# Graph convolution: 32 list entries of each step fetched as single rows by ScalarE's transfers

## The chip, the cores and the metric

The kernel runs on one core of a Trainium2 chip. The core has five engines, each with an instruction queue of its own: TensorE (PE; its weight loads are PEld) multiplies matrices, VectorE (DVE) and ScalarE (ACT) work element by element, GpSimd (POOL) issues the indirect gathers here, SyncE (SP) issues plain transfers. Transfers between the main memory and the core's memory (SBUF) run on 16 DMA engines and report on semaphores. PSUM is the small memory that TensorE writes. The metric is device time in microseconds of one execution.

## What is computed

The graph has N = 50,000 nodes with 128 features each and a list of 1,650,000 edges, sorted by destination. Each node has an edge to itself in the list. A message is one of two linear maps of the source's row, by the type of the edge; messages are summed by destination, the node's own linear map is added, then ReLU, the residual and a normalisation without scale.

```python
Xs = X[src]
m_data = Xs @ W_data.T + b_data
m_ctrl = Xs @ W_control.T + b_control
msg = jnp.where((edge_types == 0)[:, None], m_data, m_ctrl)
agg = jax.ops.segment_sum(msg, dst, num_segments=X.shape[0])
out = jax.nn.relu(agg + (X @ W_self.T + b_self))
return _layernorm(X + out, axis=-1)
```

## The kernel before

Because the maps are linear, the kernel sums source rows first, once for each edge type, and multiplies by the weights once per node. The sorted list is cut into blocks (`NBLK`, 448 of them) and each block into `Q` = 2 steps. A step has `R` = 14 chunks of 128 list entries (`SIZES`), and `F` = 53 further entries, the fillers. The entries that are a node's edge to itself need no fetch, because the block's own rows are in SBUF anyway (`xT`); `fill` puts the step's fillers at their places in the chunks, so that a gather has no idle row. A full block thus takes `BE` = 2 x (1792 + 53) = 3690 entries. Block 0 and the last one are plain: they have no fillers. The last one takes what remains of the list (`REST`, 686 entries, six chunks).

For each chunk, GpSimd issues one indirect gather of 128 rows of 512 bytes (`gathers`, line 507), at the indices in one column of an SBUF tile. VectorE builds a matrix of ones and zeros for all chunks of a block (`onehot`, line 482): row = entry, column = the destination's place in a window of 64 nodes, twice, for the two edge types. TensorE multiplies the gathered rows by it (`products`, line 530) and accumulates a step's 14 chunks in PSUM. `counts` (line 490) sums the same matrix over the chunks, for the bias terms. `add` adds the step's sums to the block's window of nodes (line 539), `layer` multiplies by the weights (lines 559 to 569), `moments`, `root` and `store` normalise (`root` is a square root on ScalarE, line 595, once for two blocks; `store` begins on VectorE with line 601), and `store_rows` writes the rows from SyncE's queue (line 609) at a row number held in a register.

The order of the work on every engine is written out by hand: within one engine, instructions run in the order in which the Python code emits them. The main loop runs over blocks b. At its start it emits the next edge lists (every ten blocks, `load_edges`, on SyncE), the adds of block b-1, then the one-hot matrix and counts of block b+2 (`AHEAD` = 2). The gathers and products of block b follow in four passes of seven chunks; between the passes stand the fillers of a later block (`fill`, lines 370 to 391, up to `RAHEAD` = 5 blocks ahead), `layer` and `moments` of block b-1, `positions` and, every ten blocks, `columns`, which prepares what ten blocks need on VectorE. The gathers of a step share one of `SLOTS` = 5 buffers and one semaphore, for which TensorE waits before the step's first product (line 514). The last block has passes of two chunks, each with a buffer of its own.

Register values are read from SBUF by a load instruction on the queue that uses them: `window` (line 458, SyncE, nine registers every eight blocks, for the transfer of line 465 and the stores) and `positions` (VectorE, four registers a block). `find_bad` makes a flag at the end; line 1006 loads it on every engine, and the path in `general` runs only where it isn't zero.

The tiles `m`, `new` and `old` of `fill` have a buffer each, of 128 partitions x (28 chunks x 63).

Of the kernel before, what the change touches and what calls it, by code (L numbers as in the profile page):

```python
# [11 lines left out]
F32 = mybir.dt.float32  # L12
BF16 = mybir.dt.bfloat16
U8 = mybir.dt.uint8
I32 = mybir.dt.int32
AF = mybir.ActivationFunctionType
ALU = mybir.AluOpType
AX = mybir.AxisListType
SP = mybir.EngineType.SP
DVE = mybir.EngineType.DVE  # L20

N = 50000
D = 128
ROW = 4 * D
E = 1650000
P = 128
# [6 lines left out]
R = 14  # L33
W = 64
Q = 2
# [3 lines left out]
F = 53  # L39
LATE = 10  # L40
FX = LATE + F
R1 = R
H = R + 1
C1 = Q * R1
SIZES = [P] * R
SIZE = sum(SIZES)
CE = Q * SIZE
BE = CE + Q * F
NBLK = 2 + (E + LATE - CE) // BE
REST = E + LATE - CE - (NBLK - 2) * BE  # L50
REST_ROWS = [min(n, max(0, REST - q * SIZE - sum(SIZES[:r]))) for q in range(Q) for r, n in enumerate(SIZES)]
# [2 lines left out]
GB = 10  # L54
GROUPS = -(-NBLK // GB)
GC = GB * C1
AHEAD = 2
SLOTS = 5
RAHEAD = 5
LOOP = 2048.0  # L60
COLS = 256
# [24 lines left out]
def plain(b):  # L86

    return b == 0 or b >= NBLK - 1
# [3 lines left out]
    return bass.AP(tensor=ap.tensor, offset=ap.offset, ap=[[0, n], *ap.ap])  # L92


def straight(ctx, tc, c, x, x_t, edges_t, edges_f, dst_first, first_p, out):

# [13 lines left out]
    eds = ctx.enter_context(tc.tile_pool(name="eds", bufs=2))  # L112
    ohp = ctx.enter_context(tc.tile_pool(name="ohp", bufs=AHEAD + 1))
    gat = ctx.enter_context(tc.tile_pool(name="gat", bufs=SLOTS))
    fil = ctx.enter_context(tc.tile_pool(name="fil", bufs=2))
    stp = ctx.enter_context(tc.tile_pool(name="stp", bufs=3))
    ps = ctx.enter_context(tc.tile_pool(name="ps", bufs=2, space=bass.MemoryType.PSUM))
# [59 lines left out]
    nc.vector.memset(stats, 0.0)  # L177
    most = keep.tile([P, GROUPS], F32, name="most")

    def load_edges(g):  # L180
        t = eds.tile([P, 3, GB, C1], I32, name="sdt", bufs=1)
        nc.sync.dma_start(t.rearrange("p m b c -> p (m b c)"), edges_t[:, g * 3 * GC:(g + 1) * 3 * GC])
        f = eds.tile([GB, 3, Q * FX], I32, name="sdt_f", bufs=1)
        nc.sync.dma_start(f.rearrange("b m f -> b (m f)"), edges_f[g * GB:(g + 1) * GB, :])
        loads[g] = {n: t[:, m] for m, n in enumerate("sdt")} | {n + "f": f[:, m] for m, n in enumerate("sdt")}


# [82 lines left out]
    def columns(g):  # L270

        a = loads.pop(g)
        first = begin[:, g * GB:(g + 1) * GB, :]
        steps = "p b (q r) -> p b q r"

# [87 lines left out]
    def fill(b):  # L363

        if plain(b):
            return
        g, i = divmod(b, GB)
        two = lists[b % 2]
        vf, cb = two[:, :Q * FX], two[:, Q * FX:]
        nc.vector.tensor_copy(cb, cb_g[g][:, i, :])  # L370
        m = fil.tile([P, C1, FX], F32, name="m", bufs=1)
        nc.vector.tensor_tensor(m, rk_g[g][:, i, :, None].to_broadcast([P, C1, FX]),  # L372
                                rank_no_ps[:, None, :].to_broadcast([P, C1, FX]), op=ALU.is_equal)
        new = fil.tile([P, C1, FX], F32, name="new", bufs=1)
        nc.vector.tensor_tensor(new.rearrange("p (q r) f -> p q r f", r=R1), m.rearrange("p (q r) f -> p q r f", r=R1),  # L375
                                vf.rearrange("p (q f) -> p q f", f=FX)[:, :, None, :].to_broadcast([P, Q, R1, FX]),
                                op=ALU.mult)
        v = fil.tile([P, C1], F32, name="v_new")
        nc.vector.tensor_reduce(v, new, AX.X, ALU.add)  # L379
        vi = fil.tile([P, C1], I32, name="vi")  # L380
        nc.vector.tensor_tensor(vi, v, stay_g[g][:, i, :], op=ALU.add)
        idx = fil.tile([P, C1], I32, name="idx", bufs=RAHEAD + 2)
        nc.vector.tensor_single_scalar(idx, vi, COLS.bit_length() - 1, op=ALU.logical_shift_right)
        nc.vector.scalar_tensor_tensor(col_g[g][:, i, :], idx, -float(COLS), vi, op0=ALU.mult, op1=ALU.add)
        idxs[b] = idx

        old = fil.tile([P, C1, FX], F32, name="old", bufs=1)
        nc.vector.tensor_tensor(old, m, cb[:, :, None].to_broadcast([P, C1, FX]), op=ALU.mult)  # L388
        by = fil.tile([P, Q, FX], BF16, name="by")
        with nc.allow_low_precision(reason="whole numbers below 256, one of them not 0"):  # L390
            nc.vector.tensor_reduce(by, old.rearrange("p (q r) f -> p q f r", r=R1), AX.X, ALU.add)  # L391
        bys[b] = by
# [43 lines left out]
    def passes_of(b):  # L436

        of = 2 if b == NBLK - 1 else PASS
        for p in range(C // of):
            q = p * of // R  # L440
            yield q, [k for k in chunks_of(b, q) if k // of == p]
# [44 lines left out]
    def counts(b):  # L486

        cnt = ohp.tile([P, Q, 2 * W], BF16, name="cnt")
        with nc.allow_low_precision(reason="whole numbers up to R1"):
            nc.vector.tensor_reduce(cnt, ohs[b].rearrange("p (q r) w -> p q w r", r=R1), AX.X, ALU.add)  # L490
        cnts[b] = cnt
# [9 lines left out]
    def gathers(b, ks):  # L501
# [13 lines left out]
        tc.declare_fence(wait.ins, group=f"rows{b}_{ks[0]}")  # L515
        return y

    def products(b, q, ks):
        of_step = chunks_of(b, q)
        if b == NBLK - 1:  # L520
            ys[b, q] = gathers(b, ks)
        elif ks[0] == of_step[0]:
            ys[b, q] = gathers(b, of_step)
        y = ys[b, q]
        if ks[0] == 0:
            accs[b] = ps.tile([P, Q, 3, W], F32, name="acc")
        acc = accs[b][:, q]
        for k in ks:
            r = REST_ROWS[k] if b == NBLK - 1 else SIZES[k % R]
            nc.tensor.matmul(acc[:, :2, :].rearrange("p t w -> p (t w)"), y[:r, k % R, :], ohs[b][:r, column(k), :],  # L530
                             start=k == of_step[0], stop=k == of_step[-1])
        if ks[-1] == of_step[-1] and q == steps_of(b)[-1]:
            for t in range(2):
                nc.tensor.matmul(accs[b][:, :q + 1, 2, :], to_row[:, t, :], cnts[b][:, :q + 1, t * W:(t + 1) * W],  # L534
                                 start=t == 0, stop=t == 1)
# [121 lines left out]
    for b in range(1, AHEAD):  # L657
        onehot(b)
        counts(b)
    made, fresh = 2, [2]  # L660
    ready = []
    for b in range(NBLK):
        if b == NBLK - 2:
            find_bad()
        if b == NBLK - 1:
            if pair(b - 2):
                store(pair(b - 2))
                ready.extend(pair(b - 2))
            while ready:
                store_rows(ready.pop(0))  # L670
        if b + 3 < NBLK:
            window(b + 3)
        g, i = divmod(b, GB)
        if i == 0 and g + 1 < GROUPS:
            load_edges(g + 1)
        due, fresh = fresh, range(made + 1, min(b + RAHEAD, made + (2 if b > GB // 2 else 1), NBLK - 1) + 1)
        made += len(fresh)
        for f in fresh:
            spread(f)
        if b > 0:  # L680
            add_all(b - 1)
        begin_sums(b)
        if b == NBLK - 1:
            layer(b - 1)
            moments(b - 1)
            root(pair(b - 1))
            own_part(b)
            store(pair(b - 1))
            for done in pair(b - 1):
                store_rows(done)  # L690
            for step, ks in passes_of(b):
                if ks:
                    products(b, step, ks)
            break
        if b + AHEAD < NBLK:
            onehot(b + AHEAD)
            counts(b + AHEAD)
        for q, (step, ks) in enumerate(passes_of(b)):
            if ks:
                products(b, step, ks)  # L700
            if q == 0:
                for f in due:
                    left_out_columns(f)
                for f in fresh:
                    fill(f)
            if q == 1 and b > 0:
                layer(b - 1)
            if q == 1:
                left_out_numbers(b + 1)
            if q == 1 and b > 0:  # L710
                moments(b - 1)
            if q == 1:
                for f in due:
                    left_out_matrix(f)
            if q == 1 and b + 1 < NBLK:
                positions(b + 1)
                left_out_rows(b + 1)
            if q == 2 and i == GB // 2 - 1 and g + 1 < GROUPS:
                columns(g + 1)
            if q == 1 and b > 1 and pair(b - 2):  # L720
                store(pair(b - 2))
                ready.extend(pair(b - 2))
            if q == 3 and b > 0 and pair(b - 1):
                root(pair(b - 1))
            if q == 3 and ready:
                store_rows(ready.pop(0))
# [231 lines left out]
def gnn_resnorm(  # L958
# [3 lines left out]
    x_t: bass.AP,  # L962
    edges_t: bass.AP,
    edges_f: bass.AP,
    dst_first: bass.AP,
    first_p: bass.AP,
    src: bass.AP,
# [34 lines left out]
             b_data=b_data, b_ctrl=b_ctrl, b_self=b_self)  # L1002

    with ExitStack() as own:
        straight(own, tc, c, x, x_t, edges_t, edges_f, dst_first, first_p, out)
    found = nc.values_load(bad, min_val=0, max_val=4 * P,
                           skip_runtime_bounds_check_because="a count of at most 3 * P + 2")
    with tc.If(found > 0):  # L1008
# [55 lines left out]
```

## Time and profile before

| | us |
|---|---|
| median of three runs | 15661.64 (15660.91 to 15671.09) |
| the profiled execution | 15668.22 |
| its span, first to last instruction | 15666.5 |
| TensorE busy | 5887.6 |
| VectorE busy | 11899.2 |
| GpSimd busy | 11833.4 |
| ScalarE busy | 69.8 |

The profile is of one execution. Busy time counts an engine's work, without register, branch, semaphore and transfer-issuing instructions; the gathers of GpSimd do count. In the lists of groups a row names line, engine and operation, then output <- input by the program's names, shapes and the count; behind the bar stand busy time in us, the mean of one in ns, and the idle time of the engine just before these instructions with what ended it. "issue" is time for which no cause is seen. A "q" behind an engine's name (ACTq, SPq, POOLq) marks what its instruction queue does itself: issue transfers, move or load registers, wait for semaphores. The duration of an issue is the time on the queue, not that of the transfer.

### The profile page before, as it was taken

The numbers are of one execution on the slowest core, as the hardware profiler recorded it, in microseconds if no ns is written. First come the engines' busy times: TensorE is split into PE (matmuls) and PEld (weight loads), VectorE is DVE, ScalarE is ACT, GpSimd is POOL, SyncE is SP. The second block draws the span as 40 slices with busy tenths as digits, with TensorE's granted clock in tenths as the row PEclk, the third lists the DMA queues.
The fourth block names the chain that finished last, engine by engine and source line by source line (L and its number), as shares of the span: only waits on it lengthen the run. The fifth ranks groups of instructions, "written<-read, shape, count | busy, mean of one in ns | idle before, by whom it ended". The sixth has DMA issues, their size and how long they took to land. (4 is left out here: it accounts for less than half of the span.)

```text
span 15666.5 us, 97614 instructions
## 1 busy us (share of the span) xinstructions
PE 5887.6 (38%) x32436; PEld 5492.1 (35%) x32437; DVE 11899.2 (76%) x12418; ACT 69.8 (0%) x231; POOL 11833.4 (76%) x12532
## 2 busy tenths in 40 slices
PE   3333333333333333333333333333333333333333
PEld 3333333333333333333333333333333333333333
DVE  9777777777777777777777777777777777777775
ACT  0000000000000000000000000000000000000000
POOL 7777777777777777777777777777777777777777
PEclk7666666666666666666666666666666666666666
DMA  2222222222222222222222222222222222222222
GB/s 61 59 57 58 57 57 59 57 60 57 57 58 57 59 57 57 59 58 59 57 57 58 57 59 57 58 58 57 58 57 57 58 57 60 57 57 58 57 59 53
DMA packets 474784, 905.35 MB, mean 58 GB/s; under 512 B 204474, under 2 KB 260873, under 8 KB 474271
## 3 DMA queue, kind: packets, MB, share of 16 engines
q0 software_dynamic: 400736, 821.40, 20.7%
q1 hardware_dynamic: 73096, 77.42, 1.7%
q8 instruction: 260, 4.26, 0.1%
q14 instruction: 254, 2.07, 0.0%
q10 hardware_dynamic: 438, 0.20, 0.0%
HBM read 869.76 MB, written 28.44 MB: 57 GB/s over the span
## 5 line engine op out<-in xcount | busy, mean ns | idle before, releaser
L507 POOL DMA_INDIRECT y<-in_x,idx x12516 | 11826.0, 945 | 3813.9 <-issue 3811.3
L530 PE MATMUL acc<-oh,y 128*128 128x128 f32 x25044 | 4965.0, 384 | 9493.2 <-PEq L514 9493.2
L530 PEld LDWEIGHTS acc<-oh,y 128*128 128x128 f32 x25044 | 4754.9, 293 | 9816.0 <-issue 5313.4
L490 DVE TENSOR_REDUCE cnt<-oh 128x256 bf16<-128x3584 f32 x448 | 2763.2, 6168 | 15.4
L482 DVE TENSOR_TENSOR oh<-col,small 128x3584 f32<-128x3584 f32 x448 | 1736.7, 3877 | 0.0
L539 DVE TENSOR_TENSOR sums<-acc,sums 128x192 f32 x895 | 319.7, 357 | 1768.7 <-PE acc L534 1749.8
L391 DVE TENSOR_REDUCE by<-old 128x126 bf16<-128x1764 f32 x446 | 1466.4, 3288 | 15.5
L370 DVE COPY small<-cb 128x28 f32<-128x28 f32 x446 | 84.1, 189 | 1547.8 <-PE small L398 1547.8
L372 DVE TENSOR_TENSOR m<-rk,small 128x1764 f32<-128x1764 f32 x446 | 888.4, 1992 | 15.2
L375 DVE TENSOR_TENSOR new<-m,small 128x1764 f32<-128x1764 f32 x446 | 888.2, 1992 | 15.2
L379 DVE TENSOR_REDUCE v_new<-new 128x28 f32<-128x1764 f32 x446 | 887.9, 1991 | 15.2
L388 DVE TENSOR_TENSOR old<-m,small 128x1764 f32<-128x1764 f32 x446 | 884.6, 1984 | 0.0
L569 PE MATMUL po<-wmsgT,sums 128*124 128x128 f32 x1792 | 315.5, 299 | 0.0
L559 PE MATMUL po<-own_w,xT 128*124 128x256 f32 x896 | 269.4, 382 | 0.8 <-DVE h L575 0.8
L555 DVE TENSOR_TENSOR sums<-pl,sums 128x372 f32<-128x372 f32 x446 | 243.2, 545 | 16.3
L569 PEld LDWEIGHTS po<-wmsgT,sums 128*124 128x124 f32 x1792 | 229.5, 187 | 54.8 <-issue 0.8
L423 DVE TENSOR_TENSOR pl<-pl,xT 128x248 f32<-128x248 f32 x446 | 189.4, 425 | 50.4 <-DVE xT L476 5.1
L567 PE MATMUL po<-bias,sums 3*124 3x128 f32 x896 | 215.1, 319 | 0.8 <-DVE sums L539 0.8
L567 PEld LDWEIGHTS po<-bias,sums 3*124 3x124 f32 x896 | 128.9, 180 | 152.1 <-issue 150.8
L406 DVE TENSOR_SCALAR z<-node_no,at 126x256 bf16<-126x256 f32 x446 | 161.0, 361 | 15.9
L361 PE MATMUL small<-v_f,row_of 74*128 74x126 bf16 x446 | 98.8, 222 | 177.7 <-DVE at L405 128.4
L476 DVE COPY xT<-xw 128x124 f32 x448 | 104.5, 233 | 79.5 <-issue 75.5
(144 smaller groups left out, 2727.9 us busy)
## 6 DMA issues: line engine op xcount, KB each, us to landing
y<-in_x,idx POOLq DMA_INDIRECT x12516
xw<-in_x_t SPq DMA_DIRECT2D x56, 496.0 KB
out<-o SPq DMA_DIRECT2D x448, 62.0 KB
sdt<-in_edges_t SPq DMA_DIRECT2D x45, 420.0 KB
sdt_f<-in_edges_f SPq DMA_DIRECT2D x45, 14.8 KB
first_i<-in_dst_first SPq DMA_DIRECT2D x1, 450.0 KB
y<-in_x,sdt POOLq DMA_INDIRECT x6
w_all<-in_L_gnn_W_data ACTq DMA_DIRECT2D x1, 64.0 KB
```

Of the source, the lines that this page charges most:

```text
L372: nc.vector.tensor_tensor(m, rk_g[g][:, i, :, None].to_broadcast([P, C1, FX]), rank_no_ps[:, None, :].to_broadcast([P, C1, FX]), op=ALU.is ...
L375: nc.vector.tensor_tensor(new.rearrange("p (q r) f -> p q r f", r=R1), m.rearrange("p (q r) f -> p q r f", r=R1), vf.rearrange("p (q f) -> ...
L379: nc.vector.tensor_reduce(v, new, AX.X, ALU.add)
L388: nc.vector.tensor_tensor(old, m, cb[:, :, None].to_broadcast([P, C1, FX]), op=ALU.mult)
L391: nc.vector.tensor_reduce(by, old.rearrange("p (q r) f -> p q f r", r=R1), AX.X, ALU.add)
L482: nc.vector.tensor_tensor(oh, col_g[g][:, i, :, None].to_broadcast([P, C1, 2 * W]), num_ps[:, None, :].to_broadcast([P, C1, 2 * W]), op=AL ...
L490: nc.vector.tensor_reduce(cnt, ohs[b].rearrange("p (q r) w -> p q w r", r=R1), AX.X, ALU.add)
L507: copy = nc.gpsimd.indirect_dma_start(out=y[:r, k % R, :].bitcast(U8), out_offset=None, in_=x_rows, in_offset=bass.IndirectOffsetOnAxis(ap ...
L530: nc.tensor.matmul(acc[:, :2, :].rearrange("p t w -> p (t w)"), y[:r, k % R, :], ohs[b][:r, column(k), :], start=k == of_step[0], stop=k = ...
L539: nc.vector.tensor_tensor(part, accs[b][:, q], part, op=ALU.add)
L567: nc.tensor.matmul(po, a[0:3, 2, :B], bias, start=False, stop=False)
L569: nc.tensor.matmul(po, a[:, t, :B], c["wmsgT"][:, t * D:(t + 1) * D], start=False, stop=t == 1)
```

## The change

Each step of a full block takes `S` = 32 more entries of the list, so that a block has 3754 entries, and there are 440 blocks. The 32 entries stand in a 15th column of the step (`R1` = 15), in the first 32 partitions. They aren't gathered by GpSimd. VectorE turns their source numbers into byte offsets every ten blocks (`offsets`), ScalarE's queue loads 32 of them into its registers at a time and issues one transfer of 512 bytes for each (`single_rows`), into one of six tiles of 32 rows. One more product of 32 rows per step adds them to the same sums, after a wait of its own. The one-hot matrix, the counts and the fillers' tiles get 15 columns a step. `old` shares the buffer of `new`. The plain blocks have no single rows; the last block has 2174 entries, 17 chunks.

```diff
+ACT = mybir.EngineType.Activation
...
-R1 = R
+R1 = R + 1
...
-BE = CE + Q * F
+S = 32
+LOAD = 32
+BE = CE + Q * (F + S)
...
+ALONE = 6
...
+    one = ctx.enter_context(tc.tile_pool(name="one", bufs=ALONE))
...
+    def offsets(g):
+        off = eds.tile([1, GB * Q * S], I32, name="off")
+        nc.vector.tensor_scalar(off, one_g.pop(g), float(ROW), float((N - 1) * ROW), op0=ALU.mult, op1=ALU.min)
+        off_g[g] = off
...
     def load_edges(g):
...
+        one = eds.tile([1, GB * Q * S], I32, name="sd1", bufs=1)
+        nc.sync.dma_start(one, edges_1[g:g + 1, :])
+        one_g[g] = one
...
     def columns(g):
...
+        offsets(g)
...
-        old = fil.tile([P, C1, FX], F32, name="old", bufs=1)
+        old = fil.tile([P, C1, FX], F32, name="new", bufs=1)
...
+    def single_rows(b):
+        if plain(b):
+            return
+        g, i = divmod(b, GB)
+        for q in range(Q):
+            j = alone_no[0] % ALONE
+            alone_no[0] += 1
+            y = one.tile([S, D], F32, name="y1")
+            for s0 in range(0, S, LOAD):
+                n = min(LOAD, S - s0)
+                at = (i * Q + q) * S + s0
+                _, regs = nc.values_load_multi_w_load_instructions(
+                    off_g[g][0:1, at:at + n], engines=[ACT], min_val=0, max_val=(N - 1) * ROW,
+                    skip_runtime_bounds_check_because=CLAMPED)
+                for k, r in enumerate(regs):
+                    r = nc.s_assert_within(r, 0, (N - 1) * ROW, skip_runtime_bounds_check_because=CLAMPED)
+                    copy = nc.scalar.dma_start(y[s0 + k:s0 + k + 1, :].bitcast(U8),
+                                               x_bytes[bass.ds(r, ROW)].rearrange("(p e) -> p e", e=ROW))
+                    copy.then_inc(alone[j], 16)
+                    tc.no_tile_sem_insts.add(copy.ins.name)
+                    tc.add_to_no_dep_group(f"single{b}_{q}", copy.ins)
+            got[j] += 16 * S
+            singles[b, q] = y, alone[j], got[j]
...
     def products(b, q, ks):
...
-                             start=k == of_step[0], stop=k == of_step[-1])
+                             start=k == of_step[0], stop=k == of_step[-1] and plain(b))
+        if ks[-1] == of_step[-1] and not plain(b):
+            y, landed_1, n = singles.pop((b, q))
+            wait = nc.tensor.wait_ge(landed_1, n)
+            tc.declare_fence(wait.ins, group=f"single{b}_{q}")
+            nc.tensor.matmul(acc[:, :2, :].rearrange("p t w -> p (t w)"), y, ohs[b][:S, q * R1 + R, :], start=False, stop=True)
...
+    for b in range(1, AHEAD):
+        single_rows(b)
     made, fresh = 2, [2]
...
             onehot(b + AHEAD)
             counts(b + AHEAD)
+        if b + AHEAD < NBLK:
+            single_rows(b + AHEAD)
```

More of the change, by code (lines that the diff above doesn't have):

```diff
@@ L92, in row_bcast, with straight @@
     return bass.AP(tensor=ap.tensor, offset=ap.offset, ap=[[0, n], *ap.ap])
-def straight(ctx, tc, c, x, x_t, edges_t, edges_f, dst_first, first_p, out):
+def straight(ctx, tc, c, x, x_t, edges_t, edges_f, edges_1, dst_first, first_p, out):
     nc = tc.nc
@@ L178, in straight @@
     most = keep.tile([P, GROUPS], F32, name="most")
+    one_g, off_g = {}, {}
+    def offsets(g):
+        off = eds.tile([1, GB * Q * S], I32, name="off")
+        nc.vector.tensor_scalar(off, one_g.pop(g), float(ROW), float((N - 1) * ROW), op0=ALU.mult, op1=ALU.min)
+        off_g[g] = off
     def load_edges(g):
@@ L516, in gathers @@
         return y
+    x_bytes = x.rearrange("n d -> (n d)").bitcast(U8)
+    alone = [tc.alloc_semaphore(f"alone{i}") for i in range(ALONE)]
+    got = [0] * ALONE
+    alone_no = [0]
+    singles = {}
+    def single_rows(b):
[21 more added lines that the diff above has]
+            singles[b, q] = y, alone[j], got[j]
     def products(b, q, ks):
@@ L964, in gnn_resnorm @@
     edges_f: bass.AP,
+    edges_1: bass.AP,
     dst_first: bass.AP,
@@ L1004, in gnn_resnorm @@
     with ExitStack() as own:
-        straight(own, tc, c, x, x_t, edges_t, edges_f, dst_first, first_p, out)
+        straight(own, tc, c, x, x_t, edges_t, edges_f, edges_1, dst_first, first_p, out)
     found = nc.values_load(bad, min_val=0, max_val=4 * P,
@@ L1029 @@
         rest = a[CE:].reshape(TBL - 1, BE)
-        steps = rest.reshape(TBL - 1, Q, SIZE + F)
+        steps = rest.reshape(TBL - 1, Q, SIZE + S + F)
         cols = np.full((TBL, Q, R1, P), pad, np.int32)
@@ L1036 @@
             cols[NBLK - 1, :, r, :n] = rest[NBLK - 2, :CE].reshape(Q, SIZE)[:, at:at + n]
+        cols[1:NBLK - 1, :, R, :S] = steps[:NBLK - 2, :, SIZE:SIZE + S]
+        if k == "src":
+            arrays["edges_1"] = np.ascontiguousarray(cols[:, :, R, :S].reshape(GROUPS, GB * Q * S))
         fills = np.full((TBL * Q, FX), pad, np.int32)
-        own = steps[:NBLK - 2, :, SIZE:].reshape((NBLK - 2) * Q, F)
+        own = steps[:NBLK - 2, :, SIZE + S:].reshape((NBLK - 2) * Q, F)
         fills[Q:(NBLK - 1) * Q, LATE:] = own
@@ L1057 @@
     with tile.TileContext(nc) as tc:
-        gnn_resnorm(tc, ap["x"], ap["x_t"], ap["edges_t"], ap["edges_f"], ap["dst_first"], ap["first_p"],
+        gnn_resnorm(tc, ap["x"], ap["x_t"], ap["edges_t"], ap["edges_f"], ap["edges_1"], ap["dst_first"], ap["first_p"],
                     ap["src"], ap["dst"], ap["edge_type_2"],
```

## The prediction, made before the changed kernel's time was known

> **What bounds the kernel now.** I read the page first: the span, the busy shares, then the costliest groups (busy time, mean of one in ns, idle time ahead of them and what ended it).
>
> ```profile
> span 15666.5 us, 97614 instructions
> ...
> PE 5887.6 (38%) x32436; PEld 5492.1 (35%) x32437; DVE 11899.2 (76%) x12418; ACT 69.8 (0%) x231; POOL 11833.4 (76%) x12532
> ...
> L507 POOL DMA_INDIRECT y<-in_x,idx x12516 | 11826.0, 945 | 3813.9 <-issue 3811.3
> L530 PE MATMUL acc<-oh,y 128*128 128x128 f32 x25044 | 4965.0, 384 | 9493.2 <-PEq L514 9493.2
> ```
>
> VectorE and GpSimd are both 76% busy, and only the idle column tells them apart. GpSimd's gathers take 11826.0 us and wait 3813.9 us, of which 3811.3 us is "issue", time without a visible cause. Together 15639.9 us over 12516 gathers: 1.2496 us a gather, nearly the whole span. The waits say the same from the other side (total, times, longest):
>
> ```profile
> POOL y L507 <- issue: 3813.1, 12516, 0.3
> DVE sums L539 <- PE acc L534: 1749.8, 392, 15.2
> DVE small L370 <- PE small L398: 1547.8, 387, 4.9
> ```
>
> Each gather has its 0.3 us, never more, so this is the price of the instruction and not a queue. VectorE waits for TensorE, and TensorE (the L530 row) 9493.2 us for the semaphore of line 514, the gathers' landing. The last question is whether GpSimd ever waits for a free slot; its line answers (min/median/max ns):
>
> ```profile
> L507 POOL DMA_INDIRECT y<-in_x,idx x12516: 940/944/1769, 3.2 to 15641.1; - x199
> L507 POOLq EVENT_SEMAPHORE  x892: 17/17/1827, 77.8 to 15632.0; - x179
> ```
>
> The median wait instruction is 17 ns. So the bound is GpSimd's count of gathers, and a block of 28 gathers lasts 28 x 1.2496 = 34.99 us.
>
> **The change, part by part.** *Gathers removed.* Blocks fall from 448 to 440 (a block now takes 2 x (1792 + 32 + 53) = 3754 entries instead of 3690). The blocks before the last lose 8 x 28 = 224 gathers: 224 x 1.2496 = 279.9 us. The last block grows: 2174 entries remain instead of 686, so 17 gathers instead of 6. Its end, from the timeline of GpSimd and the chain that ended last:
>
> ```profile
> 15642.33 0.95 POOL L507 DMA_INDIRECT y<-in_x,sdt  x1 [0.30 <-issue]
> ...
> 15648.58 1.17 POOL L507 DMA_INDIRECT y<-in_x,sdt  x1 [0.30 <-issue]
> ```
>
> ```profile
> 15641.07 2.61 DMA y<-in_x,idx
> ...
> 15653.80 2.83 PE acc L530 x12
> 15656.64 0.18 PE acc L534 x2
> ```
>
> Today the last block lasts from 15642.33 to 15666.5, 24.2 us, and its last rows (issued 15648.58) wait some 4 us for TensorE, still at the block before. With 17 gathers TensorE has caught up: the last gather starts 16 x 1.25 = 20.0 us in, lands 2.6 us later, its matmul takes 2 x 2.83/12 = 0.5 us, then the 9.9 us from 15656.64 to the end and about 0.5 us for a second add: 33.5 us. That gives back 9.3 us. With it, one half microsecond for a slot: nine passes now share five slots. Net so far -270.1 us.
>
> *VectorE's wider tiles.* The column for the single rows makes every line with 14 chunks per step 15 wide:
>
> ```profile
> L490 DVE TENSOR_REDUCE cnt<-oh 128x256 bf16<-128x3584 f32 x448 | 2763.2, 6168 | 15.4
> L482 DVE TENSOR_TENSOR oh<-col,small 128x3584 f32<-128x3584 f32 x448 | 1736.7, 3877 | 0.0
> L391 DVE TENSOR_REDUCE by<-old 128x126 bf16<-128x1764 f32 x446 | 1466.4, 3288 | 15.5
> L372 DVE TENSOR_TENSOR m<-rk,small 128x1764 f32<-128x1764 f32 x446 | 888.4, 1992 | 15.2
> L375 DVE TENSOR_TENSOR new<-m,small 128x1764 f32<-128x1764 f32 x446 | 888.2, 1992 | 15.2
> L379 DVE TENSOR_REDUCE v_new<-new 128x28 f32<-128x1764 f32 x446 | 887.9, 1991 | 15.2
> L388 DVE TENSOR_TENSOR old<-m,small 128x1764 f32<-128x1764 f32 x446 | 884.6, 1984 | 0.0
> ```
>
> 21.29 us a block in all; a fourteenth of it is 1.5 us. VectorE goes from 11899.2/448 = 26.6 to 28.1 us in a block of 35.0. Its two waits above, (1749.8 + 1547.8)/446 = 7.4 us a block, cover this: 5.9 us stay. I cost it at nothing; without that cover it would be 440 x 1.5 = 660 us. `old` taking over the buffer of `new` costs nothing either: both live on VectorE, in order.
>
> *TensorE's extra matmul* per step, two records of 0.38 us at most, plus a wait: under 1 us behind some 10 us of waiting (9493.2 us over 873 steps). Nothing; it delays VectorE's add by as much, out of the same 5.9 us.
>
> *The rows on ScalarE* decide the case. A block adds 64 transfers, each with a move of its address, and two loads of 32 registers. ScalarE is otherwise empty (69.8 us), so all of this hides while it stays under 34.99 us a block. The queue timeline of ScalarE at the start (start, duration) has three transfers of one 512-byte row:
>
> ```profile
> 1.75 0.45 ACTq L996 DMA_DIRECT2D w_all<-in_L_gnn_W_self  x1
> 2.23 0.56 ACTq L156 DMA_DIRECT2D bias<-in_L_gnn_b_data  x1
> 2.82 0.23 ACTq L156 DMA_DIRECT2D bias<-in_L_gnn_b_control  x1
> 3.09 0.26 ACTq L156 DMA_DIRECT2D bias<-in_L_gnn_b_self  x1
> ```
>
> Issue costs 0.23 to 0.56 us. I take 0.245, the mean of the last two: the first stands right behind three transfers of 128 rows and probably waits for them. No address in a register there; SyncE's lines show those, and register loads:
>
> ```profile
> L465 SPq MOVE xw<-in_x_t x56: 29/29/29, 41.9 to 15266.5; - x56
> L465 SPq DMA_DIRECT2D xw<-in_x_t x56: 348/383/392, 41.9 to 15266.5; - x56
> ```
>
> ```profile
> L458 SPq TENSOR_LOAD <-base_i x56: 959/1110/1136, 40.9 to 15265.3; - x56
> ```
>
> ```profile
> 41.95 0.35 SPq L465 DMA_DIRECT2D xw<-in_x_t  x1
> ```
>
> ```profile
> L1006 ACTq TENSOR_LOAD <-bad x1: 470/470/470, 15659.7 to 15659.7; - x1
> ```
>
> The first load ends at about 41.85 and its transfer starts at 41.95: the move with its gaps adds 0.07 to 0.14 us, I take 0.10. A load of one register takes 0.47 us, of nine 1.11: 0.08 us for each further one, so 2.95 us for 32 (bounds: 0.47, if the count is free; 32/9 x 1.11 = 3.95). A block costs 64 x 0.345 + 2 x 2.95 + half a square root of 0.30 us = 28.1 us, 6.9 below the bound. The ends: 64 x 0.30 + 0.9 = 20 us, and 64 x 0.70 + 7.9 = 52.7 us. I take the hidden side because two of three such rows were that cheap, but the upper end is far over the bound.
>
> The square root of line 595 now stands behind these transfers in ScalarE's queue. Its user, line 601 on VectorE, comes an iteration later, some 30 us; six buffers of rows let ScalarE run about two blocks ahead, so neither wait shows at 28 us a block.
>
> *Landing.* The rows of ScalarE's queue on the page:
>
> ```profile
> q10 hardware_dynamic: 438, 0.20, 0.0%
> ```
>
> 438 = 3 x (128 + 16) + 3 x 2: a single row is two packets, data and semaphore. 128 packets in 35 us, issued two blocks early, hide.
>
> *SyncE and the group work.* One more load per ten blocks on SyncE is free. `offsets` adds one VectorE operation per ten blocks, which may press on a gather beside it (timeline, line order):
>
> ```profile
> 38.42 0.61 DVE L223 TENSOR_TENSOR within<-bases_f,wide 1x448 f32<-1x448 f32 x1
> 38.48 1.37 POOL L507 DMA_INDIRECT y<-in_x,idx  x1 [0.31 <-issue]
> 38.96 1.07 DVE L224 TENSOR_TENSOR at_i<-begin,base 1x896 int32<-1x896 f32 x1
> 39.96 0.55 DVE L226 TENSOR_SCALAR at_i<-within 1x448 int32<-1x448 f32 x1
> 40.16 1.04 POOL L507 DMA_INDIRECT y<-in_x,idx  x1 [0.30 <-issue]
> ```
>
> Beside operations on two tensors a gather took 1.37 us, beside L226, which has one input like `offsets`, 1.04: 0.10 over the median. Bounds 0 and 0.43 (0 and 19 us over 44 groups); I take 0.10, 4.5 us. The Trainium skill (GPSIMD Engine Reference, 1. Specifications) says GpSimd's SBUF interfaces are shared with VectorE, in conflict with instructions of two SBUF inputs or in a two-port mode. By that rule `offsets`, if in no such mode, costs nothing, and the sum would be 4.5 us lower; the rows agree on two inputs and show a little for one.
>
> **Sum.** -279.9 + 9.3 + 0.5 + 4.5 = -265.6 us. The span goes from 15666.5 to 15400.9. The profiled execution took 15668.22 us, 1.7 more than its span; the median of the runs is 15661.64, to which I apply the difference: **15396 us**, 1.7% faster.
>
> **The rivals.** *ScalarE becomes the bound (slower).* If a transfer issued in a long row of them costs what the 128-row one cost, 0.45 us, a block takes 64 x 0.55 + 5.9 + 0.15 = 41.3 us, and 438 such blocks with 75 us for the two others and the head give 18164 us. It decides from 35.0 us a block on; at 35.6 the whole gain is gone, which is a transfer of 0.36 us, and SyncE's with a register address took 0.383. Against it: those have 128 rows, and the two undisturbed single rows took 0.23 and 0.26. Chance 0.18, because the margin is 0.11 us a transfer, and 64 in a row were never seen. The Trainium skill (DMA: Bandwidth & Descriptors, the cycle table in the section "Why a DMA increments its semaphore by 16 and not by 1") gives 512 cycles of the sequencer for a copy on generations before trn3. At the 1.2 GHz that the skill's first page (Trainium Kernel Development and Optimization, NeuronCore Architecture) gives ScalarE this is 0.43 us, an estimate by which the block would take 40 us and this rival would win; this case's 128-row transfers agree with it, its single rows at 0.23 and 0.26 don't.
>
> *Gathers get longer (most of the gain lost).* 28,032 more transfers share the DMA engines and semaphores with the gathers. Every nanosecond on a gather costs 12,309 x 0.001 = 12.3 us; 10 ns gives 15519 us, 21.6 ns no change. For it: gathers up to 1769 ns. Against it: minimum 940, median 944, mean 945, so in the steady state hardly anything touches them now. Chance 0.14.
>
> **How the numbers follow.** Forecast 0.68 (15380 to 15412), longer gathers 0.14 (15412 to 15710), ScalarE as the bound 0.18 (nearly all above 15710). The range 15380 to 15710 holds the first two, about 0.8. A measurement of this kernel tells some 0.2%, 31 us, from no change. Faster by more: 0.68 + 0.10 = 0.78. Within it: 0.03 of the second and 0.01 of the third, 0.04. Slower: 0.18.
>
> **What would show it.** Right: 12,309 gathers at a mean of 945 ns and an issue gap of 0.30 us from end to end; ScalarE's transfers of about 0.25 us and idle time of its queue in each block; VectorE near 12,360 us busy, still waiting for line 534. Wrong: GpSimd's wait for a slot in the microseconds with ScalarE's transfers back to back (first rival), or a median gather over 950 ns (second). What would make it wrong most simply is the price of one single-row transfer in a long sequence.

## The result, and the profile after

| | us | against the kernel before |
|---|---|---|
| predicted | 15396 (15380 to 15710) | 0.983 |
| measured, median of four runs | 15440.02 (15439.32 to 15440.24) | 0.9857 (95% interval 0.9845 to 0.987) |
| the profiled execution, its span | 15439.32, 15437.6 | |

The change makes the kernel 1.4% faster: 222 us between the medians, where 266 us were forecast. Between the two profiled spans it is 228.9 us of 265.6 (the profiled execution of the kernel before lay 6 us above its median). So 37 us are missing between the two traces, 44 between the medians, and the 37 are the subject of the experiments. First the page of the changed kernel: span, busy shares, and the two groups that carried the argument before (line 507 is now 523, line 530 is 576).

```profile
span 15437.6 us, 158245 instructions
...
PE 6291.5 (41%) x33627; PEld 5690.4 (37%) x33628; DVE 12401.5 (80%) x12234; ACT 68.6 (0%) x227; POOL 11669.6 (76%) x12319
...
L523 POOL DMA_INDIRECT y<-in_x,idx x12292 | 11652.1, 948 | 3748.4 <-issue 3703.3
L576 PE MATMUL acc<-oh,y 128*128 128x128 f32 x24618 | 4880.5, 384 | 8776.1 <-PEq L530 8776.1
```

GpSimd still fills the span: (11652.1 + 3748.4)/12292 = 1.2529 us a gather. Before, it was 1.2496. Most of the difference is in the gathers themselves: their mean rose from 944.9 to 947.9 ns (busy time over count), and 3.1 ns on 12292 gathers are 38 us. The idle part, 0.305 us, grew by 0.2 ns a gather, 3 us. Of these 41 us the forecast had 4.5, as the price of `offsets`. The waits show that VectorE did give up slack and still has some:

```profile
POOL y L523 <- issue: 3708.2, 12163, 0.3
DVE sums L590 <- PE acc L585: 1537.5, 363, 15.1
DVE small L386 <- PE small L414: 1039.4, 377, 4.1
```

(1537.5 + 1039.4)/438 = 5.9 us a block, as forecast. The new work on ScalarE's queue, from the instructions of lines 556 and 551 (min/median/max ns):

```profile
L556 ACTq MOVE y<-in_x x28032: 29/29/38, 16.2 to 15315.6; - x199
L556 ACTq DMA_DIRECT2D y<-in_x x28032: 227/228/534, 16.3 to 15315.6; - x199
```

```profile
L551 ACTq TENSOR_LOAD <-off x876: 2112/2240/2480, 14.0 to 15298.9; - x176
```

A single row costs 0.228 us of issue; from one row's start to the next the median is 0.318 us with the move and the gaps (worked out from the start times). A load of 32 registers takes 2.24 us. From a block's first load to the end of its last transfer, the median is 25.8 us, where 28.1 was forecast. Blocks follow each other every 34.9 us in the mean, so the queue has time left, and it spends it ahead of the square root, once in two blocks (the piece of 39.18 us holds the register loads too):

```profile
6999.83 39.18 ACTq L556 DMA_DIRECT2D y<-in_x  x97
7057.29 0.29 ACT L646 ACTIVATE sd<-mv,eps 124x2 f32<-124x2 f32 x1 [69.62 <-DVE at L421]
```

From 7039.01 to 7057.29 the queue issues nothing, 18.3 us. ScalarE is not the bound.

Where, then, do the gathers get longer? Not evenly: the median is 944 ns as before. I summed, for each of the 43 runs of `columns` inside the loop (44 before), the time over 944 ns of the gathers between 3 us before and 14 us after the memset of `h_loop`. Before: 8 us in all. After: 50 us. Outside these stretches the mean gather is 944.2 ns before and 943.8 after. The timeline shows one such stretch of each kernel, first the kernel before (start, duration; lines of other engines left out):

```profile
7181.78 0.31 DVE L288 MEMSET h_loop<- 128x300 bf16 x1
...
7182.12 0.52 DVE L289 TENSOR_TENSOR h_loop<-sdt 128x280 bf16<-128x280 int32 x1
...
7182.16 0.94 POOL L507 DMA_INDIRECT y<-in_x,idx  x1 [0.31 <-issue]
...
7185.91 0.94 POOL L507 DMA_INDIRECT y<-in_x,idx  x1 [0.30 <-issue]
...
7186.40 0.43 DVE L264 SCALAR_TENSOR_TENSOR lim<-col,last_f 128x280 f32<-128x280 f32 x1
...
7186.86 0.45 DVE L267 SCALAR_TENSOR_TENSOR v<-sdt,lim 128x280 f32<-128x280 int32 x1
...
7187.15 0.98 POOL L507 DMA_INDIRECT y<-in_x,idx  x1 [0.30 <-issue]
```

and the changed one:

```profile
7198.43 0.48 DVE L189 TENSOR_SCALAR off<-sd 1x640 int32<-1x640 int32 x1
...
7198.93 0.31 DVE L304 MEMSET h_loop<- 128x300 bf16 x1
...
7199.27 0.46 DVE L305 TENSOR_TENSOR h_loop<-sdt 128x280 bf16<-128x280 int32 x1
...
7199.34 1.19 POOL L523 DMA_INDIRECT y<-in_x,idx  x1 [0.30 <-issue]
...
7203.36 1.47 POOL L523 DMA_INDIRECT y<-in_x,idx  x1 [0.30 <-issue]
...
7203.56 0.45 DVE L279 SCALAR_TENSOR_TENSOR lim<-col,last_f 128x300 f32<-128x300 f32 x1
...
7204.05 0.47 DVE L282 SCALAR_TENSOR_TENSOR v<-sdt,lim 128x300 f32<-128x300 int32 x1
```

The operations are the same, some a little wider (`lim` 300 columns for 280, 0.45 us for 0.43). What differs is the moment: before, the gather starts 0.38 us after the memset, 0.04 us into the operation on `h_loop`, and takes 0.94 us. After, it starts 0.41 us after the memset, 0.07 us into that operation, and takes 1.19; a later one, with `lim` and `v` inside it, takes 1.47. This repeats in nearly every group, since both engines run on a fixed rhythm (the gathers every 1.25 us, `columns` a fixed chain of work after a gather's landing): 37 of the 44 groups of the kernel before have this distance at 247 to 384 ns and lose some 35 ns each, 37 of the 43 of the changed one have it at 418 to 433 and lose 1.2 us. The seven other groups of the kernel before lie at 392 ns or more, and lose 0.41 to 1.14 us: there too the later moment costs.

How a gather gets longer can be read from its end. In these stretches of the changed kernel 205 gathers take 960 ns or more, and 201 of them end 0.81 to 0.83 us after the end of one VectorE operation with two tensor inputs (on `h_loop`, `lim`, `cb`, `rk` or `col`, above all). So a gather that meets such an operation near its start seems to wait until that one has ended: the gather of 1.19 us above does so for the operation on `h_loop`, and the two-input operations that run during the rest of it add nothing. Three more end 0.12 to 0.13 us after `offsets`, which has one input.

### The profile page after: what moved, and what is told of

It reads as the page before. It is cut to its first block, busy times and chain, and to the rows that moved or that the text cites. A ratio compares the mean times of both kernels' runs of the same rounds, so it can differ in the third digit from the quotient of the medians.

```text
span 15437.6 us, 158245 instructions
## 1 busy us (share of the span) xinstructions
PE 6291.5 (41%) x33627; PEld 5690.4 (37%) x33628; DVE 12401.5 (80%) x12234; ACT 68.6 (0%) x227; POOL 11669.6 (76%) x12319
## 3 DMA queue, kind: packets, MB, share of 16 engines
q10 hardware_dynamic: 56502, 14.66, 0.4%
## 5 line engine op out<-in xcount | busy, mean ns | idle before, releaser
L523 POOL DMA_INDIRECT y<-in_x,idx x12292 | 11652.1, 948 | 3748.4 <-issue 3703.3
L576 PE MATMUL acc<-oh,y 128*128 128x128 f32 x24618 | 4880.5, 384 | 8776.1 <-PEq L530 8776.1
L506 DVE TENSOR_REDUCE cnt<-oh 128x256 bf16<-128x3840 f32 x440 | 2905.6, 6604 | 15.0
L498 DVE TENSOR_TENSOR oh<-col,small 128x3840 f32<-128x3840 f32 x440 | 1823.2, 4144 | 0.0
L590 DVE TENSOR_TENSOR sums<-acc,sums 128x192 f32 x880 | 314.2, 357 | 1553.4 <-PE acc L585 1537.5
L407 DVE TENSOR_REDUCE by<-new 128x126 bf16<-128x1890 f32 x438 | 1533.1, 3500 | 14.9
L391 DVE TENSOR_TENSOR new<-m,small 128x1890 f32<-128x1890 f32 x438 | 930.3, 2124 | 15.0
L388 DVE TENSOR_TENSOR m<-rk,small 128x1890 f32<-128x1890 f32 x438 | 930.3, 2124 | 14.9
L395 DVE TENSOR_REDUCE v_new<-new 128x30 f32<-128x1890 f32 x438 | 929.4, 2122 | 15.0
L404 DVE TENSOR_TENSOR new<-m,small 128x1890 f32<-128x1890 f32 x438 | 927.1, 2117 | 0.0
L386 DVE COPY small<-cb 128x30 f32<-128x30 f32 x438 | 83.2, 190 | 1039.4 <-PE small L414 1039.4
L582 PE MATMUL acc<-oh,y 32*128 32x128 f32 x1752 | 425.8, 323 | 0.0
L582 PEld LDWEIGHTS acc<-oh,y 32*128 32x128 f32 x1752 | 257.7, 184 | 108.0 <-issue 6.1
```

What stands on the lines that cost most here:

```text
L498: nc.vector.tensor_tensor(oh, col_g[g][:, i, :, None].to_broadcast([P, C1, 2 * W]), num_ps[:, None, :].to_broadcast([P, C1, 2 * W]), op=AL ...
L523: copy = nc.gpsimd.indirect_dma_start(out=y[:r, k % R, :].bitcast(U8), out_offset=None, in_=x_rows, in_offset=bass.IndirectOffsetOnAxis(ap ...
```

## The experiments

The kernel before was run again beside each set of runs, with medians of 15662 to 15666 us; a few us between sets are no more than that. Two theories were set against each other. A: the missing time is VectorE's `columns` work meeting the gathers at an unlucky moment, which the change moved by some ten nanoseconds. B, the prediction's own second rival: the 28,032 single-row transfers make the gathers longer.

**One memset more.** The smallest shift that theory A allows to test: nothing is taken away, one short instruction is added, on a tile of 128 x 45 numbers.

```diff
         offsets(g)
+        nc.vector.memset(late_by, 0.0)
         first = begin
```

> The changed kernel with one more VectorE instruction, a memset of 128 x 45 numbers, right behind offsets and ahead of the rest of the columns work (every ten blocks); nothing else differs. Theory A (the missing 37 us are gathers that get about 1.2 us longer in total in each run of the columns work, because they meet its two-input operations at an unlucky moment, and that moment is fixed by the chain of work before it): the gather after the first memset of h_loop starts some 50 to 90 ns less after it, near the 365 to 380 ns of the kernel before, the excess falls from about 50 us to a few, and the time from 15440 to about 15392 us, though one instruction is added. Theory B (single-row transfers lengthen the gathers): 15440 us, unchanged.

Measured: 15400.87 us (ratio to before 0.9832, 0.9818 to 0.9845), 39 us less than the changed kernel. Timeline and gather group of this kernel:

```profile
7180.85 0.10 DVE L290 MEMSET late_by<- 128x45 f32 x1
...
7180.95 0.31 DVE L306 MEMSET h_loop<- 128x300 bf16 x1
...
7181.29 0.51 DVE L307 TENSOR_TENSOR h_loop<-sdt 128x280 bf16<-128x280 int32 x1
...
7181.32 0.94 POOL L525 DMA_INDIRECT y<-in_x,idx  x1 [0.30 <-issue]
```

```profile
L525 POOL DMA_INDIRECT y<-in_x,idx x12292 | 11612.2, 945 | 3748.3 <-issue 3719.9
```

The gather now starts 0.37 us after the memset and is 0.94 us long again; the loss in these stretches is 9 us, the mean gather 945 ns. An instruction added makes the kernel faster. VectorE's wider tiles are all in this kernel too, so they don't explain the loss either. Some 0.16 us a group stay, 7 us of the 9 by which it ends above the expected 15392.

**No single rows.** In `single_rows` the loads and transfers are left out, and the product gets a tile of zeros.

```diff
-            y = one.tile([S, D], F32, name="y1")
...
-            singles[b, q] = y, alone[j], got[j]
+            singles[b, q] = none
...
-            wait = nc.tensor.wait_ge(landed_1, n)
-            tc.declare_fence(wait.ins, group=f"single{b}_{q}")
```

> The changed kernel without the single-row transfers and the register loads; the extra product multiplies a tile of zeros without a wait, so the 32 entries of each step are left out of the sums. Gathers, blocks and VectorE's work are the same. Theory A (moment of the columns work): the mean gather stays at 948 ns and the time at 15440 us, within 5. Theory B (single-row transfers lengthen the gathers): the mean gather falls to 945 ns and the time to about 15400 us.

Measured: 15437.83 us (0.9855, 0.984 to 0.987), 2 us from the changed kernel. The gathers:

```profile
L522 POOL DMA_INDIRECT y<-in_x,idx x12292 | 11649.8, 948 | 3747.4 <-issue 3703.5
```

The mean of 948 ns stays without a single transfer on ScalarE's queue; the loss in the stretches is 50 us. Theory B falls. It also prices the single rows themselves: some 2 us in the whole, no more than the sets of runs differ.

**The kernel before, moved.** If A holds, a kernel without the change must be slowed by moving its `columns` work. The tile has 128 x 980 numbers here.

```diff
         a = loads.pop(g)
+        nc.vector.memset(late_by, 0.0)
         first = begin
```

> The kernel before, with one memset of 128 x 980 numbers ahead of the columns work. It moves that work some 1.04 us later against the gathers, to where the gather starts about 580 ns after the memset of h_loop. Theory A: gathers in the columns work get about 1.0 us longer per group in total, the mean gather rises from 945 to about 948 ns, and the time rises by 35 to 45 us to about 15702 us, in a kernel without any single row; the memset itself is hidden by VectorE's slack. Theory B: 15662 us, unchanged.

Measured: 15694.51 us, 31 us slower than the kernel before (1.0019, 1.001 to 1.0028). Its gathers and a piece of its timeline:

```profile
L509 POOL DMA_INDIRECT y<-in_x,idx x12516 | 11853.2, 947 | 3814.9 <-issue 3810.9
```

```profile
7191.82 0.31 DVE L290 MEMSET h_loop<- 128x300 bf16 x1
...
7192.17 0.45 DVE L291 TENSOR_TENSOR h_loop<-sdt 128x280 bf16<-128x280 int32 x1
...
7192.35 1.08 POOL L509 DMA_INDIRECT y<-in_x,idx  x1 [0.30 <-issue]
...
7196.24 1.45 POOL L509 DMA_INDIRECT y<-in_x,idx  x1 [0.30 <-issue]
...
7196.44 0.43 DVE L265 SCALAR_TENSOR_TENSOR lim<-col,last_f 128x280 f32<-128x280 f32 x1
```

The gather starts 0.59 us after the memset of `h_loop` at the median (0.53 in the group shown), as meant; the loss is 39 us (0.9 a group), 31 more than before, and the largest part of it is again the gather beside `lim`. The direction holds, the size was expected somewhat larger.

**offsets at the end of columns.** The call moves behind the last operation of `columns`; nothing is added.

> The changed kernel with offsets at the end of the columns work instead of its head; the same instructions, none added. The rest of the columns work starts 0.48 us earlier against the gathers, so the gather after the memset of h_loop starts some 900 ns after it. Theory A (moment of the work): at that distance the kernel before lost 0.41 us in one group, so about 18 to 25 us in all instead of 50, and the time falls to about 15410 us. If the loss were the price of offsets itself, it would stay at 15440 us wherever offsets stands.

Measured: 15428.45 us (0.985, 0.9836 to 0.9863), 12 us less than the changed kernel, not 30. The gather starts 758 ns after the memset at the median, not 900, and a group loses 0.87 us, 36 in all. The place of `offsets` matters, so it isn't a fixed price; but the expected size came from one group of the kernel before, and from the belief that moving `offsets` moves the rest by its own length. The traces show where the other 142 ns went: in the changed kernel `offsets` starts 0.09 us before the operation ahead of it (`pl`) ends, and here the memset in its place starts 0.05 us after that end, so the move is about 0.33 us and not 0.48.

**Operands in PSUM.** If the loss comes from operations that read two tensors in SBUF, moving one operand to PSUM must end it where it is done, and only there. `small` and the pool `ps_c` lie in PSUM.

```diff
...
+    ones_p = small[:, 2 * W + FX + 2 * FILL + 2:][:, :1]
+    nc.vector.tensor_copy(ones_p, ones_f)
+    last_p = small[:, 2 * W + FX + 2 * FILL + 3:][:, :1]
+    nc.vector.tensor_copy(last_p, last_f)
...
-        one = ones_f[:d.shape[0], :, None] if len(d.shape) == 3 else ones_f[:d.shape[0], :]
+        one = ones_p[:d.shape[0], :, None] if len(d.shape) == 3 else ones_p[:d.shape[0], :]
...
-        lim = eds.tile(list(col.shape), F32, name="lim", bufs=1)
-        nc.vector.scalar_tensor_tensor(lim, col, 0.0, last_f[:, :, None].to_broadcast(list(col.shape)),
+        lim = ps_c.tile(list(col.shape), F32, name="lim")
+        nc.vector.scalar_tensor_tensor(lim, col, 0.0, last_p[:, :, None].to_broadcast(list(col.shape)),
```

> The changed kernel with three small operands of the columns work in PSUM instead of SBUF (the column of ones, the column of 255, and lim), so that nz, lim and v read one SBUF tensor instead of two; the other two-input operations stay. If a gather is lengthened by VectorE operations that read two SBUF tensors, the gather beside lim and v (0.53 us of the 1.2 us a group) comes back to about 0.95 us, the one beside h_loop stays at 1.18: a loss of about 28 us instead of 50, time about 15418 us. If it is any VectorE work at that moment, the loss stays near 50 us and the time at 15440 us. The moments themselves may move by some ten ns.

Measured: 15403.6 us (0.9833, 0.982 to 0.9847). From its timeline:

```profile
7181.93 1.20 POOL L528 DMA_INDIRECT y<-in_x,idx  x1 [0.30 <-issue]
...
7185.94 0.94 POOL L528 DMA_INDIRECT y<-in_x,idx  x1 [0.30 <-issue]
...
7186.14 0.45 DVE L284 SCALAR_TENSOR_TENSOR lim<-col,small 128x300 f32<-128x300 f32 x1
...
7186.63 0.47 DVE L287 SCALAR_TENSOR_TENSOR v<-sdt,lim 128x300 f32<-128x300 int32 x1
```

The distance to the memset is 0.42 us, unchanged, and the gather beside `h_loop`, which still reads two tensors of SBUF, takes 1.20 us as before. The gather with `lim` and `v` inside it, 1.47 us in the changed kernel, takes 0.94. The loss is 12 us instead of 50. The other part of the gain, beyond the expected 22 us, lies in two later gathers of each group, beside `cb` and `rk`: in the changed kernel they take 113 and 284 ns more than 944 at the median, here nothing, though these operations still read two tensors of SBUF. Those gathers now start 0.24 and 0.39 us earlier against the operations. The Trainium skill (GPSIMD Engine Reference, 1. Specifications) names this: GpSimd's SBUF interfaces are shared with VectorE, with contention when VectorE's instruction has two SBUF inputs or runs in a 2-port mode. On the two inputs these lines agree, 1.47 us with them and 0.94 without.

**48 rows a step.** How near was the first rival? `S = 48`, loaded 24 registers at a time.

> The changed kernel with 48 instead of 32 single rows a step (loaded in groups of 24 registers), 436 blocks. If ScalarE's queue costs what the changed kernel shows (0.318 us a row, 0.47 + 0.057 us a further register for a load), a block takes 96 x 0.318 + 4 x 1.78 + 0.15 = 37.8 us there, over the 35.0 us of GpSimd: 434 x 37.8 + 75 = 16480 us, slower than both kernels, with TensorE waiting for the rows. If ScalarE can run ahead or overlap more than this, GpSimd stays the bound: 12206 gathers at 1.2528 us, about 15330 us.

Measured: 17172.67 us in the profiled execution, span 17170.9; a second one took 17465.36. That is slower than both kernels, as expected, but some 700 us above the expected 16480. ScalarE's timeline, and rows of the waits and of line 551:

```profile
7000.41 27.62 ACTq L556 DMA_DIRECT2D y<-in_x  x72
7028.13 0.29 ACT L646 ACTIVATE sd<-mv,eps 124x2 f32<-124x2 f32 x1 [78.56 <-issue]
7030.03 50.03 ACTq L556 DMA_DIRECT2D y<-in_x  x122
```

```profile
DVE rstd L652 <- ACT sd L646: 4510.9, 215, 49.4
POOL y L523 <- PE acc L576: 1983.7, 277, 57.8
```

```profile
L551 ACTq TENSOR_LOAD <-off x1736: 1657/1774/1853, 14.4 to 17106.2; - x193
```

Transfers and register loads now run up to the square root and on behind it with pauses of 0.37 us at most: ScalarE is the bound. Its square roots, one for two blocks, are 78.8 us apart at the median, so a block takes 39.4 us, and 434 x 39.4 + 75 = 17175, close to the span. The estimate of 37.8 missed that the first transfer after a load takes 0.46 us instead of 0.228, and some single gaps of 0.3 us. The wait that shows isn't TensorE's for rows, as I had expected, but VectorE's for the square root that stands behind them, 4510.9 us, and GpSimd's for buffers, 1983.7 us. The mean gather is 945 ns here, with more single rows than in any other kernel: against theory B once more.

**40 rows a step.** `S = 40`, `LOAD = 20`, near the most that this price leaves room for.

> The changed kernel with 40 single rows a step, loaded 20 registers at a time: 438 blocks, 12258 gathers instead of 12309. ScalarE's queue: 80 x 0.318 + 4 x 1.98 (a load of 20 with its gaps, from the kernel with 48) + 0.15 = 33.5 us a block, still under 35.0, so GpSimd stays the bound: 51 x 1.25 = 64 us less. offsets gets 0.11 us longer, which moves the columns work to where the gather starts about 310 ns after the memset, a moment with little loss in the kernel before: another 40 to 48 us less. Together about 15332 us. If ScalarE's margin of 1.5 us is not enough in the blocks with other work, TensorE waits for rows and the time is over 15400 us.

Measured: 15383.67 us (0.9821, 0.9807 to 0.9834), 56 us less than with 32 rows, 52 above the expectation. The fewer gathers came as counted; the lucky moment did not:

```profile
7199.85 1.17 POOL L523 DMA_INDIRECT y<-in_x,idx  x1 [0.31 <-issue]
```

```profile
7200.33 0.56 DVE L189 TENSOR_SCALAR off<-sd 1x800 int32<-1x800 int32 x1
```

`offsets` lasts 0.56 us instead of 0.48, and the gather beside it grows with it, at the median from 944 to 1027 ns (the one shown is among the longest). It ends 0.12 to 0.13 us after `offsets` in 38 of the 43 groups, 0.13 in the one shown; so the next gather starts 420 ns after the memset again, and the loss is 53 us. An operation with one SBUF input can hold a gather too; which of its properties does it, no run shows.

**The two gains together.** 40 rows with the operands in PSUM, and 40 rows with the memset of 128 x 45.

> Both changes that gained, in one kernel: 40 single rows a step, and the three small operands of the columns work in PSUM. The loss in the columns work falls from 53 us to about 12, as with 32 rows: 15383.7 - 41 = about 15343 us. If the two gains overlapped, it would stay over 15360 us.

> 40 single rows a step and the memset of 128 x 45 numbers behind offsets. offsets holds the gather beside it until its own end, so the moment of the next gather is fixed by that end and the memset moves the columns work from 420 to about 365 ns: loss from 53 to about 9 us, time about 15340 us. If the moment is fixed by the longer chain before and not by offsets, the gather starts at about 290 ns, also with little loss.

Measured: 15342.46 us (0.9795, 0.9782 to 0.9809) and 15340.85 us (0.9794, 0.9781 to 0.9807). Both are what was expected, and they beat the changed kernel by 98 and 99 us. With the memset the gather starts at 366 ns in most groups, and the gather ahead of it ends 0.12 to 0.13 us after `offsets` in 39 of 43: the end of `offsets` does fix the moment in the kernel with 40 rows.

## Why the prediction was right, and what it missed

The way and the mechanism were forecast rightly: fewer gathers at a price each, with everything else hidden. The number is inside the stated range only by the width that was given to the second rival: 15440 us is above the forecast's own band (15380 to 15412) and in that rival's (15412 to 15710). With the moment moved back, the kernel with one memset more takes 15401 us, 5 us from the sum.

- *The bound* was read rightly: gathers at a fixed price, one after another. The first of the last block's 17 gathers starts at 15402.86 instead of 15642.33.
- *Gathers removed.* 224 fewer in the blocks before the last, as counted. The term failed in its price: I took 1.2496 us from the kernel before for the changed one, and it was 1.2529. Up to the last block this made 239.5 us of saving instead of 275.4 (279.9 less the 4.5 of `offsets`), and so 36 of the missing 37 us.
- *The work on offsets* was the step that should have caught it. I saw a gather of 1.37 us beside two-input operations and applied it to the new operation alone (4.5 us, at most 19). The loss sits at operations that were there already, which the change merely moved by some ten nanoseconds; here that costs 1.2 us a group, 50 us. The row that I read shows the same wait: that gather ends at 39.85, 0.82 us after the operation of line 223. That the old mean was so near the median (945 to 944) told of luck in the moment, not that nothing presses on the gathers.
- *The last block* took 34.7 us from its first gather to the end, against 33.5 + 0.5.
- *VectorE's wider tiles* stayed hidden: 12401.5 us busy against some 12,360, slack 5.9 us a block as forecast.
- *TensorE's extra product* is two records of 0.32 us, hidden.
- *ScalarE.* 0.228 us a row against 0.245 taken, 2.24 us a load against 2.95, 25.8 us a block against 28.1. The early row of 0.56 us was indeed no price of a single row. With 48 rows the rival became true, at 39.4 us a block, so the distance was real but not large.
- *The landing* was as counted; the packets of ScalarE's queue:

```profile
q10 hardware_dynamic: 56502, 14.66, 0.4%
```

  56502 = 438 + 2 x 28032.
- *The second rival* got its effect and not its cause: gathers did get longer, by 3.1 ns in the mean, but the run without any single row has the same 948 ns. Of the signs that were named, the mean of 945 ns failed, and the median of 950 for this rival didn't come either (944).

## What to carry to other kernels

Where one engine issues the same instruction without end and another works beside it on a fixed rhythm, the moment at which they meet is part of the time: look at the longest instances of the bound's instruction, not at its mean, and ask what a change of some ten nanoseconds in the other engine's chain would do to them. A test is to add a short instruction; where that makes the kernel faster, an operand moved to PSUM is the sturdier repair, since it takes the meeting away and not only the moment. And a few rows fetched one at a time from an idle queue are a good trade against a gather until that queue reaches the bound's period; what else waits in that queue, here a square root, is then what shows.

## What was not expected of the hardware

- The effect has a sharp edge, as if the one that comes first held the other back. In all these traces, a gather that starts at most 0.042 us into the two-input operation on `h_loop` takes 0.94 us, and the operation is lengthened instead (0.53 us with the gather 0.042 us into it, 0.45 alone). From 0.049 to 0.30 us, the gather is the one that waits: 1.22 us at 0.049, 1.19 at 0.08, 1.02 at 0.25, with its end about 0.82 us behind the operation's each time. So the loss jumps at the edge and falls from there.
- VectorE pays too, off the path: the shift in `fill` took 180 ns in the mean on 28 columns (line 383) and 281 ns on 30 (line 399), 181 to 394 from the 5th to the 95th percentile, and about the same without any single row (277). The trace shows what it waits for: of the 346 that took 195 ns or more, 343 started 0.52 to 0.76 us after the start of a gather and ended within 0.01 us after that gather's end. So a wait of VectorE for GpSimd exists too, for an operation with one input.
- The first transfer after a register load took 0.46 us, the others 0.228.
